# A two-layer relational graph network on one core: batches of three 14-tile chunks, the bases as stationary operand, own semaphores for the gathers

## The chip, the core and the metric

One Trainium2 chip, of which one core is used. The time is device microseconds of that core for one execution of the whole program. Lower is better.

## What is computed

Two layers of a relational graph convolution (RGCN) over 50,000 nodes with 128 features, 850,000 edges in 16 relations, then a residual and a layer norm. Cut to what matters:

```python
def _rgcn_layer(h, src, dst, rel, basis, w_comp, loop_w, bias):
    W = jnp.einsum('rb,bio->rio', w_comp, basis)
    seg = dst.astype(jnp.int32) * N_REL + rel.astype(jnp.int32)
    agg = jax.ops.segment_sum(h[src], seg, num_segments=N_ENT * N_REL)
    agg = agg.reshape(N_ENT, N_REL, -1)
    msg = jnp.einsum('nri,rio->no', agg, W)
    return jax.nn.relu(msg + h @ loop_w + bias)
...
x = _layernorm(x + layer2(layer1(x)))
```

Every relation's 128x128 matrix is a mixture of 8 bases. The edges come sorted by their target node `dst`; `src` is random. So each edge needs one row of 512 bytes, from `x` in the first layer and from the first layer's output `H1` in the second.

## The kernel before

**Tiles and chunks.** 128 edges are a tile (6641 tiles). Because targets are sorted, the edges of one tile fall into a window of `WN` = 12 successive nodes; one window position is a slot. `K` = 10 tiles are a chunk (`C` = 665 chunks), and the targets of a chunk lie in a window of 128 nodes that begins at `base_i[c]`.

**Preparation (lines 185 to 315).** Seven batches of 1024 tiles of `src` and `dst` are loaded on SP's queue, cast on ScalarE (ACT), turned on TensorE (PE) and copied by ACT, so that `src` and `key` (position of the target in its tile's window) lie with the edge on the partition. ACT's queue first issues the loads of the weights and of `first_i` (the first target of each tile, single words, lines 214 and 216); its casts and copies come after them. As soon as the first batch is turned, GpSimd (POOL) gathers the rows of the first 6 chunks (line 241). VectorE (DVE) works out `slot` and `dist` and counts whether all windows hold (`good`, line 315); line 624 branches on it to `chunked()` (line 333), the path that runs here, or to a general path that does not run.

**Gathers (helper at line 155, loop at lines 435 to 437).** One indirect DMA instruction on POOL fetches the 128 rows of one tile to `g`, 128 partitions by 128 features. There are 6 buffers of 10 tiles, used in turn. The framework gives each gather two waits: that TensorE has read the old rows, and that the gather that wrote them before has landed.

**A chunk (lines 426 to 476).** `weights()` serves four chunks at once: DVE compares the relations, laid out once for each of 16 relations over the partitions, with `its_rel` (`is_rel`, line 364), and five matmuls with `EACH` give each edge its 8 basis weights in `pm` (line 367). DVE makes `own` (which slot an edge belongs to, line 442) and `hot` = `pm` times `own`, 8 x 12 columns for each edge (line 449). For each tile TensorE multiplies the gathered rows with `hot` (line 460), summing by basis and slot at once; ACT copies five tiles' sums to `aT` (line 467).

**Finishing a chunk (lines 376 to 416),** one chunk late, after the next one's first five tiles: `slots()` has `aT` (120 columns) as the stationary operand and the basis as the moving one, 8 matmuls (line 380); a matmul with `own` (line 394) adds the slots to their nodes; a node's sum may continue in the next chunk, so each chunk adds the former chunk's sums, moved by `dist` (`shift`, `kept`, lines 396 to 400). The nodes' own rows `hw` are turned (line 163) and multiplied with `LOOP` (line 402), DVE adds the bias, and ACT's relu gives `h`, which SP writes to `H1` (line 412). In layer 2 DVE adds `xw` and works out the norm's sums, ACT scales (line 330), and SP writes to `out` (line 416). Overlapping windows are written several times; the later write holds more, so the writes wait for each other.

**Order.** A scheduler of the framework orders each engine's instructions by their dependencies; the engines run their own queues and meet through semaphores. POOL's queue holds the gathers only, so it runs ahead of TensorE by as many buffers as there are. The second layer's gathers wait for the last write of `H1`.

## Time and profile before

| what | before |
|---|---|
| median of 7 runs | 16668.5 us (16665.46 to 16670.34) |
| the profiled execution: its time, its span | 16687.22 us, 16685.4 us |
| mean granted TensorE clock | 0.678 |
| gathers (POOL DMA_INDIRECT) | 2 x 6641, mean 948 and 947 ns |
| TensorE matmul passes / weight loads | 60630 / 60630 |
| DMA | 1218.82 MB, mean 73 GB/s |
| first gather; end of the last one | 26.4 us; 16667.0 us |

A profile comes from one execution, whose time is a little over the median. "Busy" counts an engine's instructions, not its waits and not the steps between two instructions. An idle time is put down to the event that came last before it, even if the engine was not held by it; so an engine that is called idle need not have been free. An f32 matmul shows as two passes. A stretch of the span can be asked for by itself, with the busy time of each engine and the granted clock.

### The profile page before, as it was taken

The numbers are of one execution on the slowest core, as the hardware profiler recorded it, in microseconds if no ns is written. First come the engines' busy times: TensorE is split into PE (matmuls) and PEld (weight loads), VectorE is DVE, ScalarE is ACT, GpSimd is POOL, SyncE is SP. The second block draws the span as 40 slices with busy tenths as digits, with TensorE's granted clock in tenths as the row PEclk, the third lists the DMA queues.
The fourth block names the chain that finished last, engine by engine and source line by source line (L and its number), as shares of the span: only waits on it lengthen the run. The fifth ranks groups of instructions, "written<-read, shape, count | busy, mean of one in ns | idle before, by whom it ended". The sixth has DMA issues, their size and how long they took to land.

```text
span 16685.4 us, 191086 instructions
## 1 busy us (share of the span) xinstructions
PE 12985.8 (78%) x60630; PEld 11157.3 (67%) x60630; DVE 4002.5 (24%) x11719; ACT 3117.6 (19%) x8680; POOL 12581.7 (75%) x13290
## 2 busy tenths in 40 slices
PE   6777777777777777777778787777877777777777
PEld 5666666666666666666666666666666666666666
DVE  2222222222222222222222222222222222222222
ACT  2111111111111111111111221221221221221222
POOL 7777777777777777777777777777777777777777
PEclk7766666666666666666666666666666666666666
DMA  3222222222222222222222222222222222222222
GB/s 87 72 70 70 71 70 70 71 70 70 71 70 70 71 70 70 71 70 70 69 74 75 75 76 75 75 76 75 75 76 75 75 76 75 75 76 75 75 76 68
DMA packets 961778, 1218.82 MB, mean 73 GB/s; under 512 B 275684, under 2 KB 704100, under 8 KB 960768
## 3 DMA queue, kind: packets, MB, share of 16 engines
q0 software_dynamic: 425024, 871.30, 19.0%
q1 hardware_dynamic: 525876, 333.73, 6.8%
q8 instruction: 493, 8.08, 0.2%
q10 hardware_dynamic: 9868, 1.48, 0.1%
q14 instruction: 517, 4.24, 0.1%
HBM read 1118.27 MB, written 87.16 MB: 72 GB/s over the span
## 4 chain that ended last, share of the span: by engine, by line
DMA 64%; PE 19%; issue 9%; POOL 8%; POOLq 0%; ACTq 0%; ACT 0%; DVE 0%; SPq 0%
DMA g<-in_x_dram,src 33%; DMA g<-H,src 32%; PE pa L460 9%; POOL g L156 8%; PE ps L380 7%; PE po L402 1%; PE pm L367 1%; PE pn L394 1%; PE pn L398 1%; POOLq L156 0%; PE po L163 0%; ACTq L216 0%; DMA raw<-in_edges_dram 0%; ACT aT L467 0%; DMA H<-h 0%
## 5 line engine op out<-in xcount | busy, mean ns | idle before, releaser
L460 PE MATMUL pa<-hot,g 128*128 128x96 f32 x26564 | 7544.5, 386 | 3638.1 <-DMA g<-in_x_dram,src 1874.2
L460 PEld LDWEIGHTS pa<-hot,g 128*128 128x128 f32 x26564 | 5687.3, 270 | 5425.7 <-DMA g<-H,src 2294.1
L156 POOL DMA_INDIRECT g<-in_x_dram,src x6641 | 6293.2, 948 | 2048.1 <-DMA g<-in_x_dram,src 905.4
L156 POOL DMA_INDIRECT g<-H,src x6641 | 6287.7, 947 | 2036.5 <-DMA g<-H,src 856.3
L380 PE MATMUL ps<-basis,aT 128*120 128x128 f32 x21280 | 5501.4, 396 | 1.4 <-ACT aT L467 0.8
L380 PEld LDWEIGHTS ps<-basis,aT 128*120 128x120 f32 x21280 | 4578.7, 288 | 6.8 <-ACT aT L467 4.6
L467 ACT COPY aT<-pa 128x480 f32<-128x480 f32 x2658 | 1486.3, 559 | 8762.3 <-PE pa L460 8753.7
L390 DVE TENSOR_SCALAR own<-fixed,slot 120x128 f32<-120x128 f32 x1330 | 465.9, 350 | 10047.4 <-PE pn L394 10047.3
L449 DVE TENSOR_TENSOR hot<-pm,own 128x960 f32<-128x960 f32 x1330 | 1536.4, 1156 | 2012.7 <-PE pa L460 1991.0
L400 ACT COPY kept<-pn 128x128 f32<-128x128 f32 x1330 | 353.8, 266 | 2686.8 <-PE pn L398 2683.1
L402 PE MATMUL po<-loop,hT 128*128 128x128 f32 x2660 | 782.9, 389 | 4.4 <-ACT hT L165 2.8
L394 PE MATMUL pn<-slots,own 120*128 120x128 f32 x2660 | 704.3, 356 | 1.4 <-ACT slots L384 1.4
L398 PE MATMUL pn<-kept,shift 128*128 128x128 f32 x2656 | 657.7, 339 | 0.0
L367 PE MATMUL pm<-each,is_rel 128*128 128x64 f32 x3340 | 624.0, 312 | 3.4 <-DVE is_rel L364 3.4
L402 PEld LDWEIGHTS po<-loop,hT 128*128 128x128 f32 x2660 | 596.6, 276 | 25.4 <-ACT hT L165 23.8
L367 PEld LDWEIGHTS pm<-each,is_rel 128*128 128x128 f32 x3340 | 581.5, 240 | 3.7 <-issue 3.7
L394 PEld LDWEIGHTS pn<-slots,own 120*128 120x128 f32 x2660 | 556.8, 258 | 5.9 <-ACT slots L384 3.0
L398 PEld LDWEIGHTS pn<-kept,shift 128*128 128x128 f32 x2656 | 547.2, 255 | 0.2
L163 PE MATMUL po<-ident,hw 128*128 128x128 f32 x1330 | 465.6, 350 | 8.6 <-DMA hw<-H 4.4
L397 DVE TENSOR_SCALAR shift<-fixed,dist 128x128 f32<-128x128 f32 x1328 | 458.8, 345 | 42.2
L165 ACT COPY hT<-po 128x128 f32<-128x128 f32 x1330 | 354.8, 267 | 599.4 <-PE po L163 595.0
L404 DVE TENSOR_TENSOR s<-po,bias 128x128 f32<-128x128 f32 x1330 | 377.9, 284 | 294.8 <-PE po L402 282.8
(78 smaller groups left out, 3149.7 us busy)
## 6 DMA issues: line engine op xcount, KB each, us to landing
g<-in_x_dram,src POOLq DMA_INDIRECT x6641
g<-H,src POOLq DMA_INDIRECT x6641
rel<-in_edges_dram SPq DMA_DIRECT2D x332, 320.0 KB
hw<-in_x_dram SPq DMA_DIRECT2D x665, 64.0 KB
H<-h SPq DMA_DIRECT2D x665, 64.0 KB
hw<-H SPq DMA_DIRECT2D x665, 64.0 KB
xw<-in_x_dram SPq DMA_DIRECT2D x665, 64.0 KB
out_dram<-o SPq DMA_DIRECT2D x665, 64.0 KB
```

Of the source, the lines that this page charges most:

```text
L156: nc.gpsimd.indirect_dma_start(out=to, out_offset=None, in_=of, in_offset=bass.IndirectOffsetOnAxis(ap=idx, axis=0))
L163: nc.tensor.transpose(tp[:, :m], h, ident[:m, :m])
L367: nc.tensor.matmul(pm[:, :, j * NB : (j + 1) * NB], is_rel[:, j * P : (j + 1) * P], EACH[n], start=True, stop=True,)
L380: nc.tensor.matmul(ps[: k * WN], aT[:, b, : k * WN], BASIS[n][:, b, :], start=b == 0, stop=b == NB - 1)
L390: nc.vector.tensor_scalar(own[: k * WN], grid[: k * WN, :P], slot[: k * WN, c : c + 1], None, op0=OP.is_equal)
L394: nc.tensor.matmul(pn, own[: k * WN], st[: k * WN], start=True, stop=not c)
L397: nc.vector.tensor_scalar(shift, apart, dist[:, c - 1 : c], None, op0=OP.is_equal)
L398: nc.tensor.matmul(pn, shift, kept, start=False, stop=True)
L402: nc.tensor.matmul(po, turned(hw, P, sb), LOOP[n], start=True, stop=True)
L449: nc.vector.tensor_tensor(hot[:, :ks], pm[:, t0 : t0 + ks, :, None].to_broadcast([P, ks, NB, WN]), own[:, :ks, None, :].to_broadcast([P, k ...
L460: nc.tensor.matmul(pa[:, i * NB * WN : (i + 1) * NB * WN], g[:, k + i, :], hot[:, k + i].rearrange("e b w -> e (b w)"), start=True, stop=True,
L467: nc.scalar.copy(aT[:, :, k * WN : (k + m) * WN].rearrange("d b (i w) -> d i b w", w=WN), pa[:, : m * NB * WN].rearrange("d (i b w) -> d i ...
```

## The change

- A chunk has 14 tiles (`C` = 475), and three chunks are a batch (`n_done` = 159; the last batch of a layer has one chunk, of five tiles). `weights()` serves a batch, from 112 partitions with 768 columns.
- `bases_products` makes the basis the stationary operand and moves `aT` of a whole batch, 504 columns, past it: 8 matmuls a batch. The result has the slots along the columns, so `turned_back` turns it, in six parts of 7 + 1 tiles (96 slots), back to slots on partitions.
- A part also holds the 12 slots of the tile ahead of it, the last tile of the former chunk (in `sT`, with 12 columns copied from the former batch). So nodes that two chunks share get their full sum in the later one, and `shift` and `kept` remain only for the last three chunks of a layer. The preparation counts some more conditions for this, and loads `next_i` and `last_i` for them.
- The bias is a row of `sums` with ones in `own`, and `LOOP` adds into the same sums in PSUM, so that DVE's two additions go.
- The finishing of a batch is five steps, each put after a group of five tiles of the next batch. The order of the path is the program's own (`manual_schedule`).
- Seven buffers of 14 tiles. A chunk's gathers are issued in reversed order, count up one semaphore for their buffer (`landed`), and the first tile's matmul waits for all of them; the other gathers and matmuls of the chunk have no waits for rows.
- In layer 2 the last scaling is done by DVE (`tensor_scalar`), no longer by ACT.
- `key` is bfloat16. `base_i` holds byte offsets, and windows of nodes move as bytes.

The core of the diff (the new path replaces the loop of `chunked()` and its helpers):

```diff
-K = P // WN
-S = K * WN
-AT = 8
-PER = 5
-GATHERS = 6
+K = 14
+M = 3
+HALF = K // 2
+S = (HALF + 1) * WN
+AT = 7
+PER = 6
+GROUP = 5
+GATHERS = 7
...
+    SUMS = [[consts.tile([P, 2 * M, D], F32, name=f"sums{n}_{i}") for i in range(2)] for n in range(2)]
+    OWN = [consts.tile([P, 2 * M, P], F32, name=f"own{i}") for i in range(2)]
+    for n, bias in enumerate((bias1, bias2)):
+        for sums in SUMS[n]:
+            nc.scalar.dma_start(
+                sums[S : S + 1].rearrange("p (m a) d -> p a m d", a=2)[:, 0],
+                bass.AP(tensor=bias.tensor, offset=bias.offset, ap=[[D, 1], [0, M], [1, D]]),
+            )
...
-    key = consts.tile([P, n_batches * P * BATCH], F32, name="key")
+    key = consts.tile([P, n_batches * P * BATCH], BF16, name="key")
...
+            if runs // P:
+                nc.scalar.dma_start(
+                    next_i[:, : runs // P], column(1, run, [[run, P], [P * run, runs // P], [1, 1]])
+                )
+            if runs % P:
+                nc.scalar.dma_start(
+                    next_i[: runs % P, runs // P : runs // P + 1],
+                    column(1, run + runs // P * P * run, [[run, runs % P], [1, 1], [1, 1]]),
+                )
...
+            for to in (first_i[K:, 1:], last_i[:, 1:]):
+                nc.scalar.dma_start(to, column(1, (K - 1) * P, [[1, 1], [K * P, C - 1], [1, 1]]))
...
-                    if c % (AT * PER // K) == 0:
-                        pm = weights(c, n)
-                    own = hp.tile([P, K, WN], F32, name="own")
-                    nc.vector.tensor_tensor(
-                        own[:, :ks],
-                        grid[:, None, :WN].to_broadcast([P, ks, WN]),
-                        key[:, c * K : c * K + ks, None].to_broadcast([P, ks, WN]),
-                        op=OP.is_equal,
-                    )
-                    hot = hp.tile([P, K, NB, WN], F32, name="hot")
-                    nc.vector.tensor_tensor(
-                        hot[:, :ks],
-                        pm[:, t0 : t0 + ks, :, None].to_broadcast([P, ks, NB, WN]),
-                        own[:, :ks, None, :].to_broadcast([P, ks, NB, WN]),
-                        op=OP.mult,
-                    )
-                    aT = hp.tile([P, NB, S], F32, name="aT")
...
-                        if k == 0 and late is not None:
-                            kept = finish(kept, *late)
-                            late = None
-                    if late is not None:
-                        kept = finish(kept, *late)
-                    late = c, ks, aT, hw, n0, xw
-                finish(kept, *late)
...
+                def load(self):
+                    self.n0 = bases(self.c0, self.m)
+                    self.hw = twice.tile([P, M, D], F32, name="hw")
+                    self.xw = twice.tile([P, M, D], F32, name="xw") if self.n else None
+                    for j in range(self.m):
+                        nc.sync.dma_start(self.hw.bitcast(U8)[:, j, :], window(self.of, self.n0[j]))
+                    for j in range(self.m if self.n else 0):
+                        nc.sync.dma_start(self.xw.bitcast(U8)[:, j, :], window(x, self.n0[j]))
...
+                def compare(self):
+                    self.is_rel = once.tile([P, PER * P], F32, name="is_rel")
+                    nc.vector.tensor_scalar(
+                        self.is_rel[: AT * NR], self.rel[: AT * NR], its_rel[: AT * NR], None, op0=OP.is_equal
+                    )
...
+                def weights(self):
+
+                    pm = ps_m.tile([P, AT, PER * NB], F32, name="pm")
+                    for j in range(PER):
+                        nc.tensor.matmul(
+                            pm[:, :, j * NB : (j + 1) * NB],
+                            self.is_rel[: AT * NR, j * P : (j + 1) * P],
+                            EACH[self.n][: AT * NR],
+                            start=True,
+                            stop=True,
+                        )
...
+                    counts[at] += 16 * k
+                    count, name = counts[at], f"rows{self.n}_{c}"
+
+                    for t in reversed(range(k)):
+                        one = gather(g[:, t, :], self.of, src[:, c * K + t : c * K + t + 1])
+                        one.then_inc(landed[at], 16)
+                        tc.no_tile_sem_insts.add(one.ins.name)
+                        tc.add_to_no_dep_group(name, one.ins)
...
+
+                    def first(inst):
+                        inst.wait_op(landed[at], count, "sem-ge")
+                        tc.declare_no_dep(inst.ins, group=name, reason="waits for all of the rows itself")
+                        tc.declare_fence(inst.ins, group=name)
...
+                    def bases_products():
+                        ps = ps_s.tile([P, BANK], F32, name="ps")
+                        for b in range(NB):
+                            nc.tensor.matmul(
+                                ps[:, :slots], BASIS[n][:, b, :], self.aT[:, b, :slots], start=b == 0, stop=b == NB - 1
+                            )
+                        if before is None:
+                            nc.vector.memset(sT[:, :WN], 0.0)
+                        else:
+                            nc.scalar.copy(sT[:, :WN], before.sT[:, M * K * WN :])
+                        nc.scalar.copy(sT[:, WN : WN + slots], ps[:, :slots])
+                    def turned_back():
+                        nc.vector.tensor_tensor(
...
+                        pt = ps_t.tile([P, 2 * M, P], F32, name="pt")
+                        for at, s0, k in parts:
+                            nc.tensor.transpose(pt[:k, at, :], sT[:, s0 : s0 + k], ident)
+                        if whole:
+                            nc.scalar.copy(sums[:S, : 2 * m, :], pt[:S, : 2 * m, :])
...
+                    def nodes_turned():
+                        pt = ps_s.tile([P, BANK], F32, name="ps")
+                        for j in range(m):
+                            nc.tensor.transpose(pt[:, j * P : (j + 1) * P], self.hw[:, j, :], ident)
+                        self.hT = twice.tile([P, M * P], F32, name="hT")
+                        nc.scalar.copy(self.hT[:, : m * P], pt[:, : m * P])
...
+                        self.pn = ps_n.tile([P, M, D], F32, name="pn")
+                            alone = c >= C - 3
+                            mine = [p for p in parts if p[0] // 2 == j]
+                            for at, s0, k in mine:
+                                if at == 2 * j and not alone:
+                                    k += 1
+                                nc.tensor.matmul(
+                                    pn,
+                                    own[:k, at, :],
+                                    sums[:k, at, :],
+                                    start=at == 2 * j,
+                                    stop=alone and at == mine[-1][0] and c == C - 3,
+                                )
+                            if not alone:
+                                nc.tensor.matmul(
+                                    pn, self.hT[:, j * P : (j + 1) * P], LOOP[n], start=False, stop=True
+                                )
+                                continue
...
+                            if c > C - 3:
+                                shift = twice.tile([P, P], F32, name="shift")
+                                nc.vector.tensor_scalar(shift, apart, dist[:, c - 1 : c], None, op0=OP.is_equal)
+                                nc.tensor.matmul(pn, shift, handed[n][-1], start=False, stop=True)
+                            if c < C - 1:
+                                kept = twice.tile([P, D], F32, name="kept")
+                                nc.scalar.copy(kept, pn)
+                                handed[n].append(kept)
+                            po = some()
+                            nc.tensor.matmul(po, self.hT[:, j * P : (j + 1) * P], LOOP[n], start=True, stop=True)
+                            s = twice.tile([P, D], F32, name="s")
+                            nc.vector.tensor_add(s, po, BIAS[n])
+                            nc.vector.tensor_add(pn, pn, s)
...
+                    def ended():
+                        if n == 0:
+                            o = twice.tile([P, M, D], F32, name="o")
+                            nc.scalar.activation(o[:, :m, :], self.pn[:, :m, :], AF.Relu)
...
+                            for j in range(m):
+                                nc.vector.tensor_scalar(
+                                    o[:, j, :],
+                                    t[:, j, :],
+                                    mv[:, j, 0:1],
+                                    rs[:, j : j + 1],
+                                    op0=OP.subtract,
+                                    op1=OP.mult,
+                                )
+                        for j in range(m):
+                            nc.sync.dma_start(window((H1, out)[n], self.n0[j]), o.bitcast(U8)[:, j, :])
...
+            for q, batch in enumerate(batches):
+                later = batches[q + 1] if q + 1 < len(batches) else None
+                batch.load()
+                if later is not None:
+                    later.load_rel()
+                batch.aT = aT = twice.tile([P, NB, M * K * WN], F32, name="aT")
+                for t0 in range(0, batch.tiles, GROUP):
+                    pa = ps_a.tile([P, BANK], F32, name="pa")
+                    m = min(GROUP, batch.tiles - t0)
+                    for t in range(t0, t0 + m):
+                        j, k = divmod(t, K)
+                        if k == 0:
+                            hot_j = hot
+                            g, first, others = batch.fetch(j)
+                            if j == batch.m - 1 and later is not None:
+                                later.compare()
+                            if j < batch.m - 1:
+                                hot = batch.weighted(j + 1)
+                        one = nc.tensor.matmul(
+                            pa[:, (t - t0) * NB * WN : (t - t0 + 1) * NB * WN],
+                            g[:, k, :],
+                            hot_j[:, k].rearrange("e b w -> e (b w)"),
+                            start=True,
+                            stop=True,
+                        )
+                        if first is not None:
+                            (others if k else first)(one)
+                    nc.scalar.copy(
+                        aT[:, :, t0 * WN : (t0 + m) * WN].rearrange("d b (i w) -> d i b w", w=WN),
+                        pa[:, : m * NB * WN].rearrange("d (i b w) -> d i b w", i=m, w=WN),
+                    )
+                    if steps:
+                        steps.pop(0)()
+                    if later is not None and t0 <= (batch.m - 1) * K < t0 + GROUP:
+                        later.weights()
+                        hot = later.weighted(0)
+                for step in steps:
+                    step()
+                steps = batch.steps(batches[q - 1] if batch.i else None)
+                if later is None or later.n != batch.n:
```

## The prediction

> **What bounds the kernel now.** I read the engine totals first, then the queue of GpSimd (POOL), then the edges of its work in the timeline. The totals and the two costliest POOL groups (lines 460 and 380 stand between them):
>
> ```profile
> PE 12985.8 (78%) x60630; PEld 11157.3 (67%) x60630; DVE 4002.5 (24%) x11719; ACT 3117.6 (19%) x8680; POOL 12581.7 (75%) x13290
> ...
> L156 POOL DMA_INDIRECT g<-in_x_dram,src x6641 | 6293.2, 948 | 2048.1 <-DMA g<-in_x_dram,src 905.4
> L156 POOL DMA_INDIRECT g<-H,src x6641 | 6287.7, 947 | 2036.5 <-DMA g<-H,src 856.3
> ```
>
> TensorE looks busier (78%) than POOL (75%), and POOL seems to be idle for 4084 us, much of it "for a DMA". That reading is wrong, as POOL's timeline shows, first at the start (gathers that wait for nothing), then deep in the run (gathers with two semaphore waits each):
>
> ```profile
> 28.60 0.95 POOL L156 DMA_INDIRECT g<-in_x_dram,src  x1 [0.30 <-issue]
> 29.85 0.94 POOL L156 DMA_INDIRECT g<-in_x_dram,src  x1 [0.30 <-issue]
> ...
> 6002.51 0.95 POOL L156 DMA_INDIRECT g<-in_x_dram,src  x1 [0.30 <-DMA g<-in_x_dram,src]
> 6003.76 0.94 POOL L156 DMA_INDIRECT g<-in_x_dram,src  x1 [0.30 <-issue]
> ```
>
> The columns are start, duration, and in brackets the idle time before. The gap is 0.30 us in both places, whatever is named as its releaser: it belongs to the instruction. A gather costs 0.945 + 0.305 = 1.25 us of POOL with or without waits. In all 13282 gathers one gap alone is larger than 0.32 us: 13.24 us between the layers. So POOL is never waiting; the kernel is a row of gathers, back to back:
>
> 26.4 (to the first gather) + 8316.4 (layer 1's 6641) + 13.2 + 8311.0 (layer 2's 6641) + 18.4 (after the last) = 16685.4 us, the span of the profiled execution. The runs have a median of 16668.5, 17 below; I add my differences to that.
>
> The chain of waits names DMA g for 64% because rows land 2.4 us after their issue; it steps from landing to landing beside POOL. The boundary between the layers:
>
> ```profile
> 8344.72 0.55 PE L460 MATMUL pa<-hot,g 128*128 128x96 f32 x2 [1.13 <-DMA g<-in_x_dram,src]
> ...
> 8345.06 3.52 PE L380 MATMUL ps<-basis,aT 128*120 128x128 f32 x16
> ...
> 8349.58 1.92 PE L380 MATMUL ps<-basis,aT 128*12 128x128 f32 x16
> ...
> 8356.03 0.94 POOL L156 DMA_INDIRECT g<-H,src  x1 [13.24 <-DMA H<-h]
> ```
>
> Here TensorE is on the path: the last rows land at 8344.6, POOL goes on at 8356.0, 11.4 us later. The two lines of L380 also give the price of a matmul pass (f32 takes two per product): 0.22 us at the lower granted clock, 0.12 at the full one.
>
> **The change, part by part.**
>
> *Gathers.* 2 x 6641 before and after, same form. 14-tile chunks and own semaphores leave one wait where 14 gathers had two each. By the rows above a wait's price is below a nanosecond (gap 304.6 ns in the first 60, 304.7 later). Both ends: 0, or at most the 17 ns of the separate semaphore instruction that 13213 gathers carry, 225 us. I take 0: gathers without that instruction show the same gap.
>
> *Bases held in the array.* 21280 passes with as many weight loads become 318 x 16 = 5088 passes of 504 columns. Scaled from 128 columns, 504/128 x 0.12 = 0.47 us, or 0.87 at the low clock: 7.6 to 13.9 us a batch where 4.2 chunks took 67 passes, 8 to 15 us. Per batch of 42 tiles TensorE then has 84 passes of pa, these 16, 12 of pm, 9 transposes and 18 of nodes: at the low clock 123 x 0.22 + 13.9 = 41 us, where POOL needs 42 x 1.25 = 52.5. TensorE stays hidden and nothing is gained in the stream. Cover: a chunk's buffer comes round seven chunks later, 98 gathers or 122 us.
>
> *Waiting for a whole chunk, reversed gathers.* TensorE starts a chunk up to 14 x 1.25 = 17.5 us after its first row was asked for. Hidden in the stream; at the two ends of a layer it shows, below.
>
> *Head.* Eight DMA issues are added on ACT's queue (four bias rows, two next_i, two of first_i/last_i) ahead of the casts that the first gather waits for. An issue there takes 0.34 to 1.2 us; the second wave of them waits for earlier landings (the basis load issued at 8.2, say until 13.5: +2.6); 6640 single words held the next issue for 8.58 us, 1.3 ns a word, so next_i costs 1.1 + 1.1 and the last two 2.1. Sum +7; ends: 8 x 0.34 = 3, and 14 if each issue waits 1.8 us. The rest of the preparation (verdict at 69.8 us) has 98 gathers of cover instead of 60.
>
> *Boundary between the layers.* After the last landing TensorE has, in the compiled order: the rest of chunk 473 with its pm (0.6), five tiles (10 x 0.12 = 1.2), only then the bases of the batch before, 42 tiles (7.6), pm (1.4, hides ACT's copy), 6 transposes with copies of 768 and 384 columns (2.3; ACT's 480 take 0.56, 128 take 0.27), the products of three chunks, two of them a chain through kept (2.0), then the one-chunk batch: bases 16 x 0.12 = 1.9, copies and nodes 3.0: 20 us. The three writes of the former batch start at 16.5 and wait each for the one before (the H writes of before do that too: 0.35 issue + 1.5), so the fourth lands at 24.2; with 0.8 to the gather 25.0 against 11.4: **+13.5**. With the bases at the low clock +20; with writes that do not wait +10.
>
> *Tail.* The same without pm, with the norm of three chunks on DVE (3.3) ahead of the last one's; the fourth write starts at 24.0 after the landing, and before, 5.3 us passed from the last o to the end: 29.4 against 16.7, **+12.7**; ends +9, +19.
>
> *Stretched gathers.* After the first 60 gathers, 28 us are lost to gathers longer than usual; all but ten of the 168 over 0.96 us lie beside an is_rel comparison (L364, 0.55 us, SBUF to SBUF): 85 ns lost for each of 334. An element costs such an operation 0.45 ns (L244: 1024 in 0.69, L96: 128 in 0.28), so 640 are 0.29 us, of which 0.29 is lost. is_rel becomes 318 x 768 elements: 318 x 0.101 = 32, +4. New in layer 2: o as tensor_scalar on DVE instead of ACT, 475 x 0.058 x 0.29 = +8. Together **+12**. Ends: -28 (none coincide); +46 if every is_rel costs the 0.17 us of the 164 that did and every o 0.04.
>
> The Trainium skill, "SBUF — State Buffer", section "SBUF: two separate sides", says that such a DVE operation takes a port pair that GpSimd shares, for its whole length. It speaks against moving o to DVE; by it all 793 operations could cost 475 x 0.058 + 318 x 0.35 = 139 us at most, against the 40 that the rows give.
>
> **Sum**: 7 + 13.5 + 12.7 + 12 = +45 us: 16668.5 + 45 = **16714**, a span of 16730 in a profile. Ends: 3 + 10 + 9 - 28 = -6 and 14 + 20 + 19 + 46 = +99.
>
> **Rivals.**
> - *Not slower: the comparisons miss the gathers.* DVE is released by TensorE, which is released by landings, so their phase to POOL is set, not random. If they fall where the gather isn't held, -28 replaces +12: +5, **16674**, no measurable change. For: half of the 334 cost nothing. Against: the clock moves TensorE's finish from batch to batch. It decides below about 0 us of change in stretching. 0.2.
> - *Phase against it, and slow bases at both ends*: +46, +20, +19, +7: **16760**. 0.08.
> - *Faster: the waits did cost.* 225 us less, +45: **16489**. Against: the first 60 gathers. 0.04.
> - *TensorE becomes the bound*, if a batch takes it over 52.5 us with its waits for ACT copies; each us more is 318 us, at 54 us **17190**. Against: 41 us at the low clock all the time, and the clock rises when it is busy (0.80 in the first 75 us of gathers, 0.68 later). 0.03.
>
> The Trainium skill, "TensorE: Matmul & The Clock Gate", section "Part 1: The HAM clock gate", has half rate after some 3.4 us without work. With whole chunks in bursts that would make the low price the rule, also at the ends: +6 at each of the two. The trace has both prices at one boundary.
>
> **Numbers.** What a measurement can tell from no change is 0.2%, 33 us. Forecast 0.65 (own range 16690 to 16740, about 0.08 of it below 16702), rivals 0.20, 0.08, 0.04, 0.03. Faster 0.04; same 0.20 + 0.08 = 0.28; slower 0.57 + 0.08 + 0.03 = 0.68. The range: 16680 to 16755, leaving out the lower part of the first rival, the last two and a part of the second.
>
> **What would show it.** POOL's gap stays 0.30 and its groups x6641 stay near 947 ns; one gap near 27 us between the layers; first gather near 33; last gather to end near 31; weight loads of the bases line 5088; TensorE's busy share below 78%. Gathers of 0.94 with a smaller gap, or a POOL gap in mid-stream named after TensorE, would prove me wrong.

## The result, and the profile after

The changed kernel takes **16713.45 us** (median of 14 runs, 16708.4 to 16717.19) against 16668.4 (34 runs) for the kernel before: 45 us more, ratio 1.0027, 95% interval 1.002 to 1.0034. The profiled execution has a span of 16724.6 us, 39.2 more than that of before.

The engine totals, the first line of the chain of waits by engine, and the groups of the gathers and of the products with the bases, from the page of the changed kernel:

```profile
PE 9519.3 (57%) x44162; PEld 7883.8 (47%) x44162; DVE 2607.1 (16%) x3794; ACT 2290.4 (14%) x4475; POOL 12586.9 (75%) x13289
...
POOL 75%; issue 24%; PE 0%; DMA 0%; DVE 0%; ACTq 0%; ACT 0%; POOLq 0%; DVEq 0%; another core or an unknown queue 0%; SPq 0%
...
L179 POOL DMA_INDIRECT g<-in_x_dram,src x6641 | 6299.2, 949 | 2049.8 <-issue 2021.8
L179 POOL DMA_INDIRECT g<-H,src x6641 | 6287.1, 947 | 2053.5 <-issue 2022.8
...
L538 PE MATMUL ps<-aT,basis 128*128 128x504 f32 x5088 | 2654.7, 683 | 0.0
```

TensorE lost 3466 us of busy time and a quarter of its passes, VectorE and ScalarE lost instructions too, and POOL did not move. Its two groups stand where they stood, and the chain now names it outright: gathers 75%, the gap of 0.305 us after each 24%. With the separate waits gone, the trace no longer hides the row of gathers behind landings.

The span in the terms of the prediction, from the first and last gather of each layer (us):

| stretch | before | after | difference | predicted |
|---|---|---|---|---|
| to the first gather | 26.4 | 28.05 | +1.6 | +7 |
| layer 1's 6641 gathers | 8316.4 | 8322.2 | +5.8 | +12 with layer 2 |
| gap between the layers | 13.2 | 30.4 | +17.1 | +13.5 |
| layer 2's 6641 gathers | 8311.0 | 8310.1 | -0.9 | see layer 1 |
| after the last gather | 18.4 | 33.8 | +15.4 | +12.7 |

The boundary between the layers, from the timeline (start, duration, work, in brackets the idle time before):

```profile
8347.37 1.17 PE L668 MATMUL pa<-hot,g 128*128 128x96 f32 x4 [10.49 <-DMA g<-in_x_dram,src]
8348.33 2.70 PE L472 MATMUL pm<-each,is_rel 112*128 112x56 f32 x12
8350.83 4.91 PE L668 MATMUL pa<-hot,g 128*128 128x96 f32 x24
8355.99 1.33 PE L668 MATMUL pa<-hot,g 128*128 128x96 f32 x10 [0.25 <-issue]
8357.15 6.95 PE L538 MATMUL ps<-aT,basis 128*128 128x504 f32 x16
...
8371.34 1.89 PE L538 MATMUL ps<-aT,basis 128*128 128x60 f32 x16
```

```profile
8349.34 0.95 POOL L179 DMA_INDIRECT g<-in_x_dram,src  x1 [0.31 <-issue]
...
8372.79 5.90 SPq L639 DMA_DIRECT2D H<-o  x4
...
8380.65 0.94 POOL L179 DMA_INDIRECT g<-H,src  x1 [30.36 <-DMA H<-o]
```

TensorE sat idle for 10.49 us until the whole of chunk 473 had landed. Then 4 + 12 + 24 passes at 0.20 to 0.29 us each stand ahead of the last five tiles, whose rows were asked for at 8349.34; with the 2.76 us from issue to first use that the boundary of before shows (8341.85 to 8344.61), they could have begun at 8352.1 and began at 8355.99. The granted clock was 0.54 during these 40 passes and 1.00 from 8355.99 on. The bases, the other products and four writes, each waiting for the one before, follow.

At the head, ScalarE's queue (ACTq) and the first gather:

```profile
12.18 2.78 ACTq L162 DMA_DIRECT2D sums<-in_bias_dram  x4
...
15.06 0.39 ACTq L245 DMA_DIRECT2D next_i<-in_edges_dram  x1
...
15.94 0.34 ACTq L253 DMA_DIRECT2D first_i<-in_edges_dram  x1
...
16.32 5.23 ACTq L255 DMA_DIRECT2D first_i<-in_edges_dram  x1
...
22.39 0.72 ACTq L260 DMA_DIRECT2D last_i<-in_edges_dram  x1
23.14 1.28 ACT L271 ACT_TABLE_LOAD   x1 [23.14 <-DVE own L290]
...
28.05 1.09 POOL L179 DMA_INDIRECT g<-in_x_dram,src  x1 [26.76 <-ACT src L279]
```

The first gather waits for ScalarE's casts, and they start the moment its last issue ends (23.11). The added issues are there (2.78 us for the four bias rows, 0.8 for next_i), but the single words of first_i hold the queue for less. Line 253 loads 6636 of them in an issue of 0.34 us; the issue behind it, of the last five words, takes 5.23 us. In the kernel before, the issue in that place took 8.58 us:

```profile
12.89 8.58 ACTq L216 DMA_DIRECT2D first_i<-in_edges_dram  x1
```

### The profile page after: what moved, and what is told of

The parts are those of the page before. It is cut to its first block, busy times and chain, and to the rows that moved or that the text cites. A ratio compares the mean times of both kernels' runs of the same rounds, so it can differ in the third digit from the quotient of the medians.

```text
span 16724.6 us, 119274 instructions
## 1 busy us (share of the span) xinstructions
PE 9519.3 (57%) x44162; PEld 7883.8 (47%) x44162; DVE 2607.1 (16%) x3794; ACT 2290.4 (14%) x4475; POOL 12586.9 (75%) x13289
## 4 chain that ended last, share of the span: by engine, by line
POOL 75%; issue 24%; PE 0%; DMA 0%; DVE 0%; ACTq 0%; ACT 0%; POOLq 0%; DVEq 0%; another core or an unknown queue 0%; SPq 0%
POOL g L179 75%; PE ps L538 0%; PE pa L668 0%; DMA g<-in_x_dram,src 0%; DMA loop<-in_loop_w_dram 0%; DMA H<-o 0%; PE pm L472 0%; ACTq L255 0%; PE pn L584 0%; DMA ec<-in_w_comp_dram 0%; DMA g<-H,src 0%; DVE hot L485 0%; DVE pn L608 0%; DVE s L607 0%; ACTq L260 0%
## 5 line engine op out<-in xcount | busy, mean ns | idle before, releaser
L668 PE MATMUL pa<-hot,g 128*128 128x96 f32 x26564 | 5071.0, 362 | 7134.6 <-DMA g<-H,src 3610.8
L668 PEld LDWEIGHTS pa<-hot,g 128*128 128x128 f32 x26564 | 4765.0, 272 | 7452.2 <-DMA g<-H,src 3695.5
L485 DVE TENSOR_TENSOR hot<-pm,own_w 128x1344 f32<-128x1344 f32 x950 | 1477.7, 1556 | 12565.1 <-PE pa L668 6961.8
L677 ACT COPY aT<-pa 128x480 f32<-128x480 f32 (+1 forms) x2846 | 1508.4, 533 | 11926.0 <-PE pa L668 11753.5
L538 PE MATMUL ps<-aT,basis 128*128 128x504 f32 x5088 | 2654.7, 683 | 0.0
L538 PEld LDWEIGHTS ps<-aT,basis 128*128 128x128 f32 x5088 | 1142.8, 232 | 1302.5 <-issue 1302.5
L472 PE MATMUL pm<-each,is_rel 112*128 112x56 f32 x3816 | 856.5, 414 | 7.7 <-DMA hw<-in_x_dram 7.7
L472 PEld LDWEIGHTS pm<-each,is_rel 112*128 112x128 f32 x3816 | 849.7, 332 | 8.2 <-issue 8.2
L584 PE MATMUL pn<-sums,own 97*128 97x128 f32 (+1 forms) x3796 | 813.1, 353 | 4.9 <-DVE own L548 2.5
L584 PEld LDWEIGHTS pn<-sums,own 97*128 97x128 f32 (+1 forms) x3796 | 738.6, 271 | 6.2 <-ACT hT L570 3.0
```

Source lines behind the costliest of these rows:

```text
L472: nc.tensor.matmul(pm[:, :, j * NB : (j + 1) * NB], self.is_rel[: AT * NR, j * P : (j + 1) * P], EACH[self.n][: AT * NR], start=True, stop ...
L485: nc.vector.tensor_tensor(self.hot[:, :k], self.pm[:, t0 : t0 + k, :, None].to_broadcast([P, k, NB, WN]), self.own[:, t0 : t0 + k, None, : ...
L538: nc.tensor.matmul(ps[:, :slots], BASIS[n][:, b, :], self.aT[:, b, :slots], start=b == 0, stop=b == NB - 1)
L584: nc.tensor.matmul(pn, own[:k, at, :], sums[:k, at, :], start=at == 2 * j, stop=alone and at == mine[-1][0] and c == C - 3,)
L668: one = nc.tensor.matmul(pa[:, (t - t0) * NB * WN : (t - t0 + 1) * NB * WN], g[:, k, :], hot_j[:, k].rearrange("e b w -> e (b w)"), start= ...
L677: nc.scalar.copy(aT[:, :, t0 * WN : (t0 + m) * WN].rearrange("d b (i w) -> d i b w", w=WN), pa[:, : m * NB * WN].rearrange("d (i b w) -> d ...
```

## The experiments

All are compared with the kernel before on the same chip in the same call. The first call's chip ran the kernel before in 16698.0 us, the second's in 16669.6, so differences are compared: +45 for the changed kernel, measured in a call of its own.

| run | time | before, same call | difference | ratio, 95% interval |
|---|---|---|---|---|
| e1_framework_waits | 16747.4 | 16698.0 | +49 | 1.0018 to 1.0041 |
| e2_bases_twice | 16765.7 | 16698.0 | +68 | 1.0027 to 1.0058 |
| e3_o_on_act | 16743.0 | 16698.0 | +45 | 1.0016 to 1.0038 |
| e4_psum_compare | 16723.8 | 16698.0 | +26 | 1.0008 to 1.0026 |
| e5_loads_on_sp | 16712.5 | 16669.6 | +43 | 1.0016 to 1.0035 |
| e6_13_of_14 | 15551.2 | 16669.6 | -1118 | 0.9314 to 0.9343 |
| e7_small_last | 16711.4 | 16669.6 | +42 | 1.0015 to 1.0035 |
| e8_after_all | 16691.3 | 16669.6 | +22 | 1.0004 to 1.0022 |

The intervals are some 15 to 26 us wide to each side, so differences of a few us between runs rest on the traces, not on the times.

### Is the row of gathers the floor? (e6_13_of_14)

```diff
-                    counts[at] += 16 * k
+                    counts[at] += 16 * (k - 1)
-                    for t in reversed(range(k)):
+                    for t in reversed(range(1, k)):
```

> The changed kernel, one gather of each chunk left out (the rows of one tile in fourteen are not fetched again, so that tile works on rows of an older one); all else stays. Theory (the stream is a row of gathers of 0.945 + 0.305 us, and nothing else sets it): 942 or 943 gathers fewer of the 13282 by layer pairs, 948 x 1.25 = 1185 us at most, 1170 to 1185 us below the changed kernel, so 1125 to 1140 us below the kernel before. Rival (TensorE or the rows' landings set the stream): less than half of that, and gaps between gathers in mid-stream named after TensorE.

```profile
L179 POOL DMA_INDIRECT g<-in_x_dram,src x6173 | 5855.9, 949 | 1908.2 <-issue 1880.4 <-ACT src L279 27.2 <-PE pa L668 0.3
L179 POOL DMA_INDIRECT g<-H,src x6166 | 5834.2, 946 | 1912.2 <-issue 1878.5 <-DMA H<-o 33.3 <-DMA g<-in_x_dram,src 0.3
```

These are its two groups: 12339 gathers instead of 13282, with mean, gap and releaser as before. The 943 left out are worth 943 x 1.25 = 1179 us; the time is 1163 below the changed kernel (-1118 against +45), a little less than the 1170 expected, the ends being 7 us longer in this trace (33.3 and 37.9). The floor is shown: per gather, layer 1 took 1253 ns in both kernels, layer 2 1251. A gather left out also takes its transfer away, but the transfers don't set the pace: in the changed kernel's page their queue keeps the DMA engines busy for 19% of the span, and the rows land 2.5 us (median) after the issue.

### Did the waits cost anything? (e1_framework_waits)

The row semaphores are taken out; the framework's own waits are back.

```diff
+                    for t in reversed(range(k)):
+                        gather(g[:, t, :], self.of, src[:, c * K + t : c * K + t + 1])
+                    return g, None, None
```

> The changed kernel without its own semaphores: every gather again waits for the gather whose semaphore it takes over, and every matmul of rows waits by itself; chunks, batches and order stay. Theory (POOL's gathers are back to back at 1.25 us and the wait is inside that): 16713, within 10 us, gap before a gather 0.305 us. Rival (the waits cost POOL the 17 ns of their semaphore instruction, and the changed kernel gained that and lost it elsewhere): 16713 + up to 225 = 16940.

+49 against +45, and a mean gap of 304.8 ns between gathers against 304.7. But this kernel carries only 946 separate semaphore instructions on POOL, so the run could show no more than 946 x 17 ns = 16 us of the rival. The traces of before, after and e1 together show the rest (count, then ns of the shortest, the median and the longest):

```profile
L156 POOLq EVENT_SEMAPHORE  x13213: 17/17/43, 101.8 to 16658.7; - x198
...
L179 POOLq EVENT_SEMAPHORE  x9: 17/17/17, 254.4 to 8379.9; - x9
...
L179 POOLq EVENT_SEMAPHORE  x946: 17/17/43, 156.1 to 16662.7; - x190
```

With 13213 of them and with 9, the mean gap is 304.7 ns. The rival by which the waits cost falls.

### Is TensorE hidden, and what do the bases cost at the ends? (e2_bases_twice)

```diff
+                        for i in range(2):
                             for b in range(NB):
                                 nc.tensor.matmul(
```

> The changed kernel with the bases' products done twice (the second set overwrites the first, so the result is the same): 5088 more passes of 504 columns, 0.42 us each at the full clock, at least 2140 us more work on TensorE. Theory (TensorE hidden in the stream, open only after the last landing of each layer): 7 us more at each of two ends, 16727. Rival (TensorE is near to being the bound): some hundreds to 2100 us more.

The group of the bases, then the boundary, in its page and timeline:

```profile
L539 PE MATMUL ps<-aT,basis 128*128 128x504 f32 x10176 | 4778.6, 632 | 0.0
```

```profile
8352.97 14.42 PE L539 MATMUL ps<-aT,basis 128*128 128x504 f32 x32
...
8376.66 6.92 PE L539 MATMUL ps<-aT,basis 128*128 128x60 f32 x32
```

The bases work 2124 us more (TensorE in all 1292 more, as its other passes got shorter: granted clock 0.75 against 0.69), and the kernel takes 23 us more. Of these, 14.2 are in the gap between the layers (44.60) and 9.6 after the last gather (43.43): all of it at the ends, nothing in the stream. The second set cost 7.5 us for the big batch, as expected. The small batch went from 1.89 to 6.92, but not all of that is the second set: its passes run at 0.22 us each here (6.92 / 32, granted clock 0.50), at 0.12 in the changed kernel, and in e1, which has no second set, its 16 passes took 3.51 us, 0.22 each. So the second set is nearer to 7.5 + 3.4 = 11 us at this end than to the 7 expected, and what the small batch costs changes from one execution to another.

### Which VectorE operations hold gathers up? (e3_o_on_act, e4_psum_compare)

e3 puts the last step of the norm back on ScalarE:

```diff
-                                nc.vector.tensor_scalar(
-                                    o[:, j, :],
...
+                                nc.scalar.activation(
+                                    o[:, j, :], t[:, j, :], AF.Identity, bias=nm[:, j : j + 1], scale=rs[:, j : j + 1]
```

> The changed kernel with the last scaling of layer 2 on ACT again (bias and scale as in the kernel before) instead of tensor_scalar on DVE. My prediction charged the 475 DVE operations with 8 us of stretched gathers: by it 16705. By the trace of the changed kernel, in which gathers beside o alone are not longer: no more than 1 or 2 us, 16712.

+45, as without the edit: the 475 o operations cost nothing that the time shows. Its interval would hide a few us, and the traces show some: in layer 2 the time lost to long gathers is 10.3 us here and 14.6 in the changed kernel's. e4 leaves the comparison where it is and takes one operand from PSUM:

```diff
+    rel_of = fixed[:, 2, 0:1]
+    nc.vector.tensor_copy(rel_of, its_rel)
...
-                    nc.vector.tensor_scalar(
-                        self.is_rel[: AT * NR], self.rel[: AT * NR], its_rel[: AT * NR], None, op0=OP.is_equal
+                    nc.vector.tensor_tensor(
+                        self.is_rel[: AT * NR],
+                        self.rel[: AT * NR],
+                        rel_of[: AT * NR].to_broadcast([AT * NR, PER * P]),
+                        op=OP.is_equal,
```

> The changed kernel with is_rel made by tensor_tensor against its_rel in PSUM, so that one of DVE's two operands does not come from SBUF; 318 operations get longer. Theory (the comparison holds up the gather's descriptor writing when both lie in SBUF): the 27 us of stretched gathers after the first 60 go to below 5, time 16713 - 25 = 16688. Rival (any DVE operation beside a gather stretches it, or the longer operation more so): 16713 or more.

The comparison in the changed kernel and in e4:

```profile
L456 DVE TENSOR_SCALAR is_rel<-rel,its_rel 112x768 f32<-112x768 int32 x318 | 202.4, 637 | 6.8 <-DMA rel<-in_edges_dram 6.8
...
L458 DVE TENSOR_TENSOR is_rel<-rel,fixed 112x768 f32<-112x768 int32 x318 | 301.0, 947 | 6.9 <-DMA rel<-in_edges_dram 6.9
```

The comparison itself became slower, 947 ns in this group against 637, and the kernel 19 us faster than the changed one. Time lost to gathers over 0.955 us, after the first 60, fell from 27.2 us to 3.9. That is 0.073 us for each of the 318: the comparison with both operands in SBUF is what stretches gathers, not VectorE's time as such. The edit changes the operation's form along with the operand's place, so e4 alone does not tell the two apart. Other rows speak for the place: hot, a tensor_tensor of 1.56 us with one operand in PSUM, lengthened 1 of the 1884 gathers beside it in e4 by over 10 ns, while operations of the preparation with all operands in SBUF, two of the three a tensor_tensor too, held one gather for 4.14 us (shown below).

Most of what is left in e4 belongs to o. Gathers of layer 2 that begin while an o runs (121) lose 2.6 of the 3.9 us, up to 0.11 us each. Those that were already running when an o began (127), and those that begin inside a comparison (92), lose nothing. One that does, behind the third of three o:

```profile
8686.99 0.86 DVE L635 TENSOR_SCALAR o<-t,mv,rs 128x128 f32<-128x128 f32 x3
...
8687.65 1.02 POOL L181 DMA_INDIRECT g<-H,src  x1 [0.31 <-issue]
8687.76 0.95 DVE L458 TENSOR_TENSOR is_rel<-rel,fixed 112x768 f32<-112x768 int32 x1
```

So o cost some 3 to 4 us (an estimate from e3 and e4), about half of the 8 that the prediction charged.

The Trainium skill, "SBUF — State Buffer", section "SBUF: two separate sides", has the shared port pair as an exclusive lock that whichever starts first keeps "for the whole instruction". The PSUM run agrees on the cause. For the size it gives only a bound: by whole operations 318 x 0.637 = 203 us would be the most (an estimate), and 23 are lost. In layer 2 of the changed kernel 67 gathers begin inside a comparison; they lose 9.6 us together, and none over 0.40 us.

### What releases the first gather? (e5_loads_on_sp)

```diff
-            nc.scalar.dma_start(first_i[:K, : n_tiles // K], column(1, 0, [[P, K], [K * P, n_tiles // K], [1, 1]]))
+            nc.sync.dma_start(first_i[:K, : n_tiles // K], column(1, 0, [[P, K], [K * P, n_tiles // K], [1, 1]]))
```

and the same for the other loads of next_i, first_i and last_i.

> The changed kernel with its loads of next_i, first_i and last_i issued by SyncE's queue instead of ScalarE's. Theory (the first gather waits for ScalarE, whose casts stand behind these issues: 5.2 us for the first_i words alone in its queue): first gather near 20 us instead of 28.05, time 8 us below the changed kernel, 45 - 8 = 37 us above the kernel before on the same chip. Rival (the gather waits for the landing of src itself, the order of issues is nothing): first gather stays near 28, +45.

```profile
3.34 0.39 SPq L253 DMA_DIRECT2D first_i<-in_edges_dram  x1
...
5.00 12.92 SPq L245 DMA_DIRECT2D next_i<-in_edges_dram  x1
...
21.50 3.79 ACTq L162 DMA_DIRECT2D sums<-in_bias_dram  x4
...
25.31 1.28 ACT L271 ACT_TABLE_LOAD   x1 [25.31 <-DMA ec<-in_w_comp_dram]
...
30.24 1.10 POOL L179 DMA_INDIRECT g<-in_x_dram,src  x1 [28.95 <-ACT src L279]
```

This missed: the first gather came later, at 30.24. ScalarE's queue was free of the loads, but its second wave of issues now ended at 25.29 instead of 14.96. On SyncE the scheduler put the 6636 words of first_i ahead of next_i, and the issue behind them took 12.92 us; in that time ScalarE's second wave stood still for some 8 us (from 11.86 to 19.61). That the single words hold up landings in the other queue as well is inferred from this, not shown. The casts still start when ScalarE's queue is done. The order was tried instead of the queue below, in e11.

### Where did the smaller last batches' gain go? (e7_small_last, e8_after_all)

```diff
-    n_done = -(-C // M)
+    sizes = [M] * ((C - 4) // M)
+    sizes += [1] * (C - sum(sizes))
+    n_done = len(sizes)
```

with the batch's first chunk and size read from sizes.

> The changed kernel, in which the last four chunks of each layer are batches of one chunk, all others still three. Theory (the two ends pay for a batch of 42 tiles whose bases, transposes and four serial writes stand behind the last rows): the gap between the layers falls from 30.4 to about 22, the end after the last gather from 33.8 to about 26, time 16 us below the changed kernel, +29 against the kernel before. Rival (the ends are the serial writes and the one-chunk chain alone, not the batch): both stay within 3 us, +42 to +45.

```profile
8361.22 0.36 SPq L641 DMA_DIRECT2D H<-o  x1
...
8362.52 0.89 SPq L447 DMA_DIRECT2D rel<-in_edges_dram  x1
...
8367.66 0.62 DVE L458 TENSOR_SCALAR is_rel<-rel,its_rel 112x768 f32<-112x768 int32 x1 [6.77 <-DMA rel<-in_edges_dram]
...
8368.33 2.81 PE L474 MATMUL pm<-each,is_rel 112*128 112x56 f32 x12 [4.78 <-DVE is_rel L458]
...
8384.67 0.95 POOL L181 DMA_INDIRECT g<-H,src  x1 [32.96 <-DMA H<-o]
```

+42: the rival was nearer. The gap between the layers stayed (32.96), the end shortened by 3 us (30.78). In the five traces whose ends have no edit (the changed kernel, e1, e3, e4, e5) the gap is 30.4 to 34.0 and the end 33.8 to 36.4, so only the end lies outside what the same code shows. The big batch of bases is gone from the chain, and a new wait took its place: rel has one buffer, its next load, for the first batch of layer 2, is queued on SyncE behind the H write of a batch that isn't finished, the comparison waits 6.77 us for it, and TensorE 4.78 for the comparison. After that wait the granted clock is 0.50, and the last chunk's bases take 3.51 us instead of 1.89. A batch of three had its rel long before.

e8 joins e4, e5 and e7:

> The changed kernel with three edits together: is_rel compared with a number in PSUM, the loads of next_i, first_i and last_i on SyncE's queue, the last four chunks of a layer as batches of one. Theory (each term of the sum stands by itself on GpSimd's row of gathers): -19 (measured for the first), -8, -16, so 45 - 43 = +2 us against the kernel before, no measurable difference. Rival (the terms hide one another): +15 or more.

+22, the rival's side. But the terms do add up, with what they measured: 45 - 19 - 2 - 3 = +21. What fell is the size of the last two, each of which is well inside its interval.

### Four runs in which the gathers were not the floor (e9 to e12)

e9 is the kernel before with the PSUM comparison and the first_i load behind the first cast; e10 is e7 with rel loaded on ScalarE's queue; e11 is the changed kernel with the loads of next_i, first_i and last_i moved behind the first casts in the program; e12 joins e4, e10 and e11. In load_rel (e10 and e12), and behind the casts in the loop over i (e11 and e12; e9 with its two loads of first_i), the edits are:

```diff
-                        nc.sync.dma_start(
+                        nc.scalar.dma_start(
...
+            if i == 0:
+                with nc.allow_non_contiguous_dma(reason="one word in P"):
...
+                    nc.scalar.dma_start(first_i[:K, : n_tiles // K], column(1, 0, [[P, K], [K * P, n_tiles // K], [1, 1]]))
```

> The kernel before with two edits: is_rel compared with a number held in PSUM, and the load of first_i put behind the casts that the first gather waits for. Theory (a comparison with both operands in SBUF holds gathers beside it up; the first gather waits for ScalarE's queue): -20 to -27 for the first, -6 to -10 for the second, 26 to 37 us below the kernel before, the fastest of all. Rival for the second edit (something else releases the first gather): -20 to -27 alone, first gather still near 26.

> The changed kernel with the last four chunks of each layer as batches of one, as in the run before it, and the rel loads on ScalarE's queue instead of SyncE's. Theory (with small batches the loads of rel for the next batch stood behind the H and out writes on SyncE's queue, and the comparison that waits for them, at 8367.66 in that run, took the gain): that comparison comes 4 us earlier or more, gap between the layers 25 to 29, end 26 to 29, time 6 to 12 us below that run, +30 to +36 against the kernel before. Rival (the chain of one-chunk batches itself is as long as the big batch): no more than 2 us below that run.

> The changed kernel with the loads of next_i, first_i and last_i behind the first casts in ScalarE's order. Theory (their issues, 7.7 us from 15.06 to 23.11 on ScalarE's queue, hold the first gather): first gather near 20.5 instead of 28.05, +37 against the kernel before. Rival (the landing of something else releases the casts, and the last run, with those loads on SyncE, had no gain for that reason): first gather above 26, +43 to +45.

> The changed kernel with all three: PSUM comparison (-19 measured), loads behind the first casts (-7.5), one-chunk batches at the layers' ends with the rel loads on ScalarE's queue (-8 to -14). Theory (the terms add up on GpSimd's row of gathers): 45 - 19 - 7.5 - 11 = +8, from +3 to +12 against the kernel before. Rival (they hide one another, as the three of the run before did, +22): +15 or more.

The chip of this call ran the kernel before in 19566 us, 17% more than in the other calls. e9 took 19564 (0.999 to 1.0008), e10 19764 (1.0085 to 1.0116), e11 19751 (1.0081 to 1.0112), e12 19754 (1.008 to 1.011). What POOL waited for in e11 (us in total, times, longest):

```profile
POOL g L179 <- issue: 3857.1, 12652, 0.6
POOL g L179 <- PE pa L669: 2188.0, 309, 16.3
...
POOL g L179 <- remote: 949.0, 313, 10.2
```

A gather costs the same there (944 ns and 0.30), but 627 times in mid-stream POOL stops for some 5 us, about half of the times until TensorE gives a buffer back (the others the trace puts down to an unknown releaser), and TensorE is busy for 46% only. e9 stops 2296 times, more briefly. So there the gathers are not the floor, e9's edits had nothing to gain, and kernels with the changed batches lose 1%. The rows are not what comes late: the last packet of a gather ends 2.1 us after the gather's start (median), in e11 as in the changed kernel. Which resource is slower on that chip isn't settled: the trace names "another core or an unknown queue" for 59% of the chain and holds few of the landings.

One reading carries over, as it lies before the stream. The head of e11:

```profile
15.00 1.28 ACT L252 ACT_TABLE_LOAD   x1 [15.00 <-DMA sums<-in_bias_dram]
...
16.30 1.04 ACT L252 CAST srcf<-raw 128x1024 f32<-128x1024 int32 x1
...
19.41 3.52 ACTq L275 DMA_DIRECT2D first_i<-in_edges_dram  x1
...
19.92 2.12 POOL L179 DMA_INDIRECT g<-in_x_dram,src  x1 [18.64 <-ACT src L260]
```

The first gather comes at 19.92 instead of 28.05 (in the same call 27.25 in e10, which leaves the loads in place, and 20.14 in e12, which moves them): it is the order on ScalarE that holds it, as the prediction had it. In e9 the same move did nothing (26.72), and for the same reason: an 11.79 us issue of first_i fell between the two casts that the gather needs. e10's and e12's question stays open, and whether the kernel before with e4's comparison beats 16668 was not measured where gathers are the floor; from e4, some 20 us would be the estimate.

## Why the prediction held, step by step

The time came out as forecast, 16713 for 16714. The mechanism held; that the number did to 1 us is luck, as four terms were off by 3 to 7 us, two each way, and 6 us are in none of them.

- **POOL is the floor, waits are free, TensorE is hidden**: right, by e6, by the gaps of before, after and e1, and by e2. 3466 us less TensorE work bought nothing in the stream.
- **Head, +7; measured +1.6**, below its lower end of 3. The mechanism is right (e11), the size is off: "next_i costs 1.1 + 1.1 and the last two 2.1" took 0.80 and 1.48, and the issue behind the words of first_i, counted as unchanged, got 3.35 us shorter.
- **Boundary, +13.5; measured +17.1.** The mis-sized term is "the rest of chunk 473 with its pm (0.6)". Waiting for a whole chunk left 40 passes after its landing, and they ran at the low clock (0.54 granted; 0.205 us a pass of pa, 0.225 of pm); the last tiles began 3.9 us after they could. At 0.12 us a pass, 40 passes from 8347.37 on would have ended at 8352.2, as the last rows came: so it is the clock that made the term (an estimate from these rows). The rest held: bases 6.95 for 7.6, small batch 1.89 for 1.9, 7.9 from the first write to the gather for 8.5.
- **Tail, +12.7; measured +15.4.** Here the last tiles began 2.1 us after they could (16694.73 against 16689.85 + 2.76), and the last o came 24.4 us after that landing. The failed term is "the fourth write starts at 24.0": four writes took 7.75 us to issue, 2.5 apart, so that the fourth left at 27.2 and the end came 7.55 us after the last o, not 5.3:

```profile
16689.85 0.94 POOL L179 DMA_INDIRECT g<-H,src  x1 [0.30 <-issue]
...
16712.41 7.75 SPq L639 DMA_DIRECT2D out_dram<-o  x4
...
16716.70 0.35 DVE L630 TENSOR_SCALAR o<-t,mv,rs 128x128 f32<-128x128 f32 x1 [0.37 <-DVE rs L627]
```

- **Stretched gathers, +12; measured +5.** The +8 for o on DVE was too much: it cost some 3 to 4 us (e3, e4). After the first 60, all long gathers together lost 27.2 us, o's share included, against 28, so the comparison's +4 did not come either. What did come was not in the sum: in the first 60 gathers 14.2 us were lost instead of 8.0, beside the added VectorE work of the preparation:

```profile
46.77 1.21 DVE L289 TENSOR_TENSOR own<-rel,most 128x1024 f32<-128x1024 f32 x1
...
46.93 4.14 POOL L179 DMA_INDIRECT g<-in_x_dram,src  x1 [0.30 <-issue]
...
47.90 1.21 DVE L269 TENSOR_TENSOR rel<-raw,tb 128x1024 f32<-128x1024 int32 x1
...
49.03 1.22 DVE L290 SCALAR_TENSOR_TENSOR own<-rel,own 128x1024 f32<-128x1024 f32 x1
```

  One gather beside three such operations in a row took 4.14 us instead of 0.945.
- The Trainium skill, "TensorE: Matmul & The Clock Gate", section "Part 1: The HAM clock gate", has TensorE at half rate after a few microseconds without work, and the prediction put +6 to each end by it, outside its sum. The trace agrees: 10.49 us without work, then 40 passes at a granted clock of 0.54, then 1.00. These passes took 8.4 us where 0.12 us each would be 4.8, so about 3.6 us of the 6 came at the boundary, and the 2.1 us at the tail have the same 40 passes ahead of them. Left out of the sum, this is the larger part of what the boundary missed.
- **Sum**: 1.6 + 17.1 + 15.4 + 4.9 = 39.0, but for rounding the 39.2 of the profiled executions; the medians differ by 45, 6 more, as the profiled executions lie 19 us (before) and 13 us (after) above them.
- **The rivals**: "comparisons miss the gathers" fell (27 us still lost), TensorE as the bound did not come in the first three calls; in the fourth, on the slow chip, something of its kind did.

## What to carry to other kernels

When a view names landings or TensorE for a queue's idle time, compare the gap with one from a place where nothing is awaited: if it is the same, the queue itself is the floor, and only instructions taken from that queue, its head and its ends can be won or lost. Coarser batches that are free in the stream are paid in full at every end, and passes that follow an idle wait run at the low clock (0.50 to 0.54 granted here); price the ends pass by pass from the last landing, with the backlog that a whole-chunk wait leaves. Before a batch is made smaller at an end, look at what is prefetched for it and in which queue that load stands.

## What the runs showed of the hardware

- A VectorE comparison of 112x768 with both operands in SBUF lost 0.073 us of gather time each. With one operand in PSUM it took 947 ns instead of 637, and the 92 gathers of layer 2 that began inside it lost nothing. Operations o, of 128 columns from SBUF to SBUF, cost gathers that began while one ran up to 0.11 us in e4 (121 gathers, 2.6 us) and those already running nothing (127). Three 1024-column operations in a row held one gather for 4.14 us.
- The same gather has slightly different lengths in different executions: the median is 944 ns in the traces of e1, e2, e6 and e8 and 947 in those of e3, e4, e5 and e7. Over 13282 gathers 2.3 ns make 30 us, about the distance between the first two chips' times of the kernel before. It also parts executions of one call: e1's profiled one (944) took 16713 us, the other six 16744 to 16750; e5's (947) took 16742, the other nine 16708 to 16715.
- The issue that follows a load of 6636 or 6640 single words in the same queue took 5.23 us (after), 8.58 (before), 11.79 (e9), 3.52 (e11), and on SyncE 12.92 (e5), though it moved 1 to 768 words itself: an issue's length says what it waits for, not how much it moves. What makes it longer or shorter was not tested.
- After 10.49 us without work TensorE's granted clock was 0.54 for 8.4 us, then 1.00. The 16 passes of the same small batch took 1.89 us in one execution (0.12 each) and 3.51 in another (0.22 each).
- The chip of one call ran the same program 17% slower with unchanged gathers and a granted clock (0.71) no lower than elsewhere.
